# Layer 0 of a sparse graph network: the packed edges' own rows by a float32 one-hot product instead of by row fetches

## The chip, the cores and the metric

The kernel runs on one core of a Trainium2 chip. The metric is device time in microseconds (us) of one execution; a kernel is run several times and the median is told. The engines of the core work side by side, each through its own instructions in their order: PE (matmul; PEld is its weight load), DVE (vector), ACT (scalar, activation functions), POOL (here it issues indirect DMAs) and SP (issues plain DMAs). DMAs of all engines share 16 DMA engines.

## The reference, cut to what matters

Four layers work on x (4096 nodes, 64 features) with one adjacency matrix (4096 x 4096, an edge with probability 0.000976562, so about 4 edges a row). Each layer is x = x + layer(relu(layernorm(x))). Layer 0 is the one that is changed:

```
h = relu(layernorm(x))
left, right = logmap0(h) @ w_att[:64], logmap0(h) @ w_att[64:]
att[i, j] = sigmoid(left[i] + right[j] + b) * adj[i, j]
support[i] = sum_j att[i, j] * logmap(h[i], h[j])     # hyperbolic logarithm
x = x + proj(expmap(h, support))
```

logmap(h[i], h[j]) needs the products h[i].h[j], h[i].h[i] and h[j].h[j] and then only scalars, so an edge (i, j) costs the two rows h[i] and h[j], their dot product, and some 40 scalar operations. Layers 1 to 3 multiply the adjacency (as 8-bit floats) with 64 columns, on PE.

## The kernel before, in words

**Layer 0 by edges.** The function `neighbours` makes lists of edges and fetches rows of a table for them. The table `tab` has one row per node with TW = 69 columns: h (64), then scalars (1 + c x2, x2, right part, floor, left part). It lies in SBUF, as 32 tiles of 128 nodes, one node a partition, and a copy `rows_d` in HBM is what the fetches read.

**Stream.** 64 tiles of the transposed adjacency, 1 MB each, are loaded by SP into four buffers (`load`, L602). For each, ACT casts it to 8 bits (L800 for the first 24 tiles, which stay in SBUF; L803 for 40 tiles, which go through the buffers `f8` to HBM, L804, since SBUF is full of layer 0's tiles; they are loaded back at L1406 when layer 0 has ended), and PE packs it: the matmuls `pk` (L808) turn 16 rows of adjacency bits into one number. Eight tiles make a block: 512 nodes, in LB = 4 tiles of 128. After each half block ACT moves the packed words to `kt` (L814), PE transposes them (L818), and ACT copies a whole block's into `keyt` (L831).

**Lists (`lists`, one per block, NR = 8).** On DVE, eight-maximum and replace operations (L853 to L893) find a node's edges in the packed words. Up to NS = 4 edges of a node go to slots; `idx` (L879) holds the rows of their other ends, and `gather_slots` has POOL issue LB x NS = 16 indirect DMAs, one row per partition in each (`fetch`, L962), into `es`. Edges beyond the slots, up to NV = 24 a partition, are packed over partitions: PE counts them with a triangular matrix (`pb`, L901 and L902), DVE makes `mine` (L911), a one-hot matrix of 128 partitions by 512 places that tells from which partition each packed place takes its edge, and PE multiplies `mine` with the list's numbers (`pc`, L920 and L921). `mine` and the numbers are bfloat16, the numbers split into a high half `mvh` (L903) and a low half `mvl` (L904), two matmuls for each of NO = 4 columns of places. DVE then works out for each packed place `ovx`, the row of its edge's other end (L933), `own`, the row of the node it belongs to (L935, L936), and `rows_at`, where its result is to be added (L940, L941). `gather_packed` issues 2 x NO = 8 further fetches: 4 for `ovx` into `es`, 4 for `own` into `hi`.

**The rest of a block.** `chunk` forms the dot products: for the slots h is read from `tab` (L993), for the packed places from `hi` (L1005); ACT copies x2 and left of the nodes beside them (L999 from `tab`, L1003 from `hi`). `weights` computes the scalars of two blocks at a time (of the last two blocks one at a time), `sums` scales the fetched rows (L1115) and has PE add them up, `products`: slots with the identity (L1090), packed places with one-hot matrices `spot` (L1073, L1097). `dots` and `finish` end the layer for a group of rows (a group is two blocks; `finish` runs once for the first two groups and once for the last two), and write x (L1233). `row_stage` makes the table at the start, `row_rest` six small operations after it (L780 to L785) that only `finish` needs.

**The order.** Inside layer 0 the order of instructions on PE, DVE, ACT and POOL is fixed when the program is written. A planner runs a clock with assumed costs: each job is a generator that emits some instructions and yields their planned time in us on DVE (a bare number), PE or ACT, or the fetch queue ("FETCH"). STREAM_AT, PACE_MB and LATE say when tiles are assumed to arrive, ROWS_AT when the row stage has ended, PACE_DMA what a fetch costs (1.25), LANDED how long after the last fetch a chunk may be placed. Jobs are taken in the order of `kinds`, lists first if the fetch queue has under BACKLOG us of work. When PE has nothing planned, `fill` puts matmuls (L1083) that compute nothing of use there, into the PSUM bank `fill_t`.

Of the kernel before, what the change touches and what calls it, by code (L numbers as in the profile page):

```python
# [17 lines left out]
P = 128  # L18
# [32 lines left out]
STREAM_AT, PACE_MB, LATE = 8.0, 3.9, 3.0  # L51
ROWS_AT, PACE_DMA, LANDED, BACKLOG, SLOW, AHEAD, FILL = 46.0, 1.25, 3.0, 12.0, 1.05, 0.6, 0.75
EARLY = 3
# [524 lines left out]
def neighbours(ctx, tc, x_in, x, sh, adj_t, adj8, a8, over):  # L578
# [74 lines left out]
    V.tensor_scalar(upto, sh.diff, 0.0, None, op0=ALU.is_ge)  # L653


    mvh = [l0.tile([P, NV + 3], BF16, name=f"mvh{s}") for s in range(2)]
    mvl = [l0.tile([P, NV + 1], BF16, name=f"mvl{s}") for s in range(2)]
    for s in range(2):
        V.tensor_scalar_mul(mvh[s][:, NV + 1 : NV + 2], p_f, float(NCH))
        V.tensor_scalar_add(mvh[s][:, NV + 2 :], p_f, 1.0)  # L660

    def scalar(name):
# [60 lines left out]
    def row_stage(beside):  # L723
# [38 lines left out]
        V.tensor_scalar_mul(pn, x2, c_t)  # L762
        V.tensor_scalar(tab[:, :, D + 3], pn, NOISE2, RSQRT_MIN, op0=ALU.mult, op1=ALU.add)
        for m in range(NQ):
# [3 lines left out]
        V.tensor_mul(la, la, iv)  # L768
        V.tensor_mul(tab[:, :, D + 2], right, la)
        V.tensor_mul(left, left, la)  # L770
        V.tensor_scalar_add(tab[:, :, D + 4], left, sh.batt_t)
        nc.scalar.dma_start(rows_d[1:, :].rearrange("(p n) w -> p n w", p=P), tab)
# [5 lines left out]
    def row_rest():  # L778

        V.tensor_scalar(beta, x2, negc_t, 1.0, op0=ALU.mult, op1=ALU.add)  # L780
        V.tensor_scalar_max(clipb, beta, MIN_NORM)
        V.tensor_scalar_mul(fac, clipb, 3.0 / 16.0)
        V.tensor_mul(fb, fac, beta)
        V.reciprocal(rcb, clipb)
        V.tensor_scalar_mul(rcb, rcb, rc_t)  # L785


# [3 lines left out]
    def pack(u):  # L791
# [4 lines left out]
        for v in range(4):  # L796
            at = part * 4 + v
            a = load(b, at)
            if b < EARLY:
                S.copy(a8[b][:, 4 * at : 4 * at + 4, :], a, saturate=False)  # L800
            else:
                f8 = strm.tile([P, 4, 512], FP8, tag="f8", bufs=3, name=f"f8_{b}_{at}")
                S.copy(f8, a, saturate=False)  # L803
                nc.scalar.dma_start(adj8[b][:, 4 * at : 4 * at + 4, :], f8.bitcast(BF16))  # L804
            bits = a.bitcast(BF16).rearrange("p j (i b) -> p j i b", b=2)
            for j in range(4):
                w = 4 * v + j
                T.matmul(  # L808
                    pk, wflat[:, w * P : (w + 1) * P], bits[:, j, :, 1], start=(w == 0), stop=(w == 15),
                )  # L810
            if v < 3:
                yield
# [22 lines left out]
    ovx = [l0.tile([P, NO], U32, name=f"ovx{b}") for b in range(NR)]  # L835
    own = [l0.tile([P, NO], U32, name=f"own{b}") for b in range(NR)]
    rows_at = [l0.tile([P, NO], F32, name=f"rows_at{b}") for b in range(NR)]

    k16s = l0.tile([P, NR, LB, 16], F32, name="k16s")
    vfs = l0.tile([P, NR, LB, 16], F32, name="vfs")  # L840
    ovs = l0.tile([P, NR, NV], F32, name="ovs")
    ends = l0.tile([P, NR], F32, name="ends")
    BIG = 1.5 * 2.0**36

    def lists(nb):
        def tile_(tag, shape, dt=F32):
            return l0e.tile([P] + shape, dt, tag=tag, name=f"{tag}_{nb}")

        k16, vf, ov = k16s[:, nb], vfs[:, nb], ovs[:, nb]
        scr = tile_("scr", [NW])  # L850
# [44 lines left out]

        cnt, om, mh, ml = tile_("cnt", [1]), tile_("om", [NV]), mvh[nb % 2], mvl[nb % 2]
        V.tensor_scalar(om, ov, 0.0, None, op0=ALU.is_gt)
# [4 lines left out]
        T.matmul(pb[:, 1:2], upto, cnt, start=True, stop=True, skip_group_check=True)  # L902
        V.tensor_copy(mh[:, :NV], ov)  # L903
        V.tensor_sub(ml[:, :NV], ov, mh[:, :NV])  # L904
        yield 0.4
        yield "PE", 0.5

        at0, end = pb[:, 0:1], pb[:, 1:2]
        from_, mine = tile_("from", [512], BF16), tile_("mine", [512], BF16)
        V.tensor_scalar(from_, io, at0, None, op0=ALU.is_gt)  # L910
        V.scalar_tensor_tensor(mine, io, end, from_, op0=ALU.is_le, op1=ALU.mult)  # L911
        V.tensor_copy(mh[:, NV : NV + 1], at0)
        V.tensor_sub(ml[:, NV:], at0, mh[:, NV : NV + 1])
        V.tensor_copy(ends[:, nb : nb + 1], end)
        yield 1.7
        pc = psum.tile([P, 512], F32, tag="s", bufs=1, name=f"pc{nb}")
        pe = pc[:, : NO * (NV + 3)].rearrange("p (c e) -> p c e", c=NO)
        for c in range(NO):
            at = mine[:, c * P : (c + 1) * P]
            T.matmul(pe[:, c, :], at, mh, start=True, stop=False, skip_group_check=True)  # L920
            T.matmul(pe[:, c, : NV + 1], at, ml, start=False, stop=True, skip_group_check=True)  # L921
        yield "PE", 1.0

        tf, c1, kt_, rw, rw2 = (tile_(t, [NO]) for t in ("tf", "c1", "kt_", "rw", "rw2"))
        its = tile_("its", [NO, NV])
# [8 lines left out]
        V.tensor_scalar(kt_, c1, BIG, -1.0 / 8192.0, op0=ALU.subtract, op1=ALU.mult)  # L934
        V.scalar_tensor_tensor(rw, kt_, float(1 + LB * nb), pe[:, :, NV + 1], op0=ALU.add, op1=ALU.add)  # L935
        V.scalar_tensor_tensor(own[nb], tf, 0.0, rw, op0=ALU.is_gt, op1=ALU.mult)  # L936
        yield 0.9
        gather_packed(nb)
        yield "FETCH", PACE_DMA * 2 * NO
        V.scalar_tensor_tensor(rw2, kt_, float(P), pe[:, :, NV + 2], op0=ALU.mult, op1=ALU.add)  # L940
        V.scalar_tensor_tensor(rows_at[nb], tf, 0.0, rw2, op0=ALU.is_gt, op1=ALU.mult)  # L941
        yield 0.35

# [14 lines left out]
    NE = LB * NS + NO  # L958
    es, hi, s_e, x2e, lfe = {}, {}, {}, {}, {}

# [5 lines left out]
    def gather_slots(nb):  # L966
        g, q = divmod(nb, 2)
        if q == 0:
            es[g] = l0w.tile([P, 2, NE, TW], F32, tag="es", name=f"es{g}")
            hi[g] = l0w.tile([P, 2, NO, TW], F32, tag="hi", name=f"hi{g}")  # L970
        for k in range(LB):
            for s in range(NS):
                fetch(es[g][:, q, k * NS + s, :], idx[nb][:, k, s : s + 1])

    def gather_packed(nb):
        g, q = divmod(nb, 2)
        for c in range(NO):
            fetch(es[g][:, q, LB * NS + c, :], ovx[nb][:, c : c + 1])
        for c in range(NO):
            fetch(hi[g][:, q, c, :], own[nb][:, c : c + 1])  # L980

    def chunk(nb):
# [14 lines left out]
        )  # L997
        for dst, col in ((x2e, D + 1), (lfe, D + 4)):
            S.copy(  # L999
                dst[g][:, q, :ns].rearrange("p (k s) -> p k s", k=LB),  # L1000
                tab[:, tiles, col : col + 1].to_broadcast([P, LB, NS]),
            )
            S.copy(dst[g][:, q, ns:], own_[:, :, col])  # L1003
        yield 1.2
# [4 lines left out]
    def weights(se, e_g, x2i, lf, name, last):  # L1009
# [7 lines left out]

        xj, right, floor = e_g[:, :, :, D + 1], e_g[:, :, :, D + 2], e_g[:, :, :, D + 3]
        den, gap, pr, y, e, w = (tile_(t) for t in ("den", "gap", "pr", "y", "e", "w"))
# [56 lines left out]
    pieces = []  # L1076
    fill_t = psum.tile([P, 512], F32, tag="fill", name="fill_t")
    fill_in = io.bitcast(BF16)[:, :512]

    def fill(n):  # L1080

        for _ in range(n):
            T.matmul(fill_t, wflat[:, :P], fill_in, start=True, stop=True, skip_group_check=True)  # L1083
# [156 lines left out]
    with tc.manual_schedule(engines=engines):  # L1240
        units = [pack(u) for u in range(2 * NR)]
        packed = [0]
        clock = {"now": ROWS_AT, "FETCH": ROWS_AT + 6.0, "PE": 0.0, "ACT": 0.0}

# [21 lines left out]
        row_stage(pack_one)  # L1266
        row_rest()
        landed, freed, done = {}, {}, set()
# [18 lines left out]
        def freed_by(nb):  # L1287

            return [("sum", nb // 2 * 2 - 1)] if nb > 1 else []

        class Job:
            def __init__(self, kind, nb, gen, ready, end=None):
# [10 lines left out]

        kinds = ["chunk", "sum", "last", "spot", "list", "dots", "finish", "over"]
        queues = {k: [] for k in kinds}
        for nb in range(NR):
            g, q = divmod(nb, 2)
            queues["list"].append(Job("list", nb, lists(nb), list_ready, list_done))
            queues["chunk"].append(Job("chunk", nb, chunk(nb), landed.get))
            queues["spot"].append(Job("spot", nb, spots(nb), after(("list", nb), *freed_by(nb))))  # L1310
# [9 lines left out]
        for g0, g1 in ((0, NQ - 2), (NQ - 2, NQ)):  # L1320
            queues["finish"].append(Job("finish", g0, finish(g0, g1), after(*[("dots", g) for g in range(g0, g1)])))
        queues["over"].append(Job("over", 0, overflow(0), after(("list", NR - 1))))
# [454 lines left out]
```

## Time and profile before

| | us |
|---|---|
| median of 5 runs | 941.34 |
| lowest, highest | 940.16, 946.19 |
| the profiled execution: whole time | 947.1 |
| the profiled execution: span, first to last instruction | 945.2 |
| mean granted clock of TensorE in it | 0.897 of full |
| busy of the span: PE, PEld, DVE, ACT, POOL | 764.2, 569.2, 496.0, 343.7, 202.3 |
| first and last fetch on POOL begin | 61.99, 313.81 |
| last write of x in layer 0 ends (L1233) | 360.9 |

How to read it: times in the views count from the span's start. A row of a timeline gives start, duration, engine, line, operation, output <- inputs, shape, how often, and in brackets how long the engine had been idle and what ended that. The busy tenths have one digit for each of 40 equal slices. A row of the waits gives who waited for what: us in total, times, longest. A matmul with float32 operands shows as two records.

### The profile page before, as it was taken

How to read it: one execution, taken by the hardware profiler on the slowest of the kernel's cores; microseconds unless marked ns; L12 is line 12 of the kernel's file. 1: busy time of each engine (PE TensorE's matmuls, PEld its weight loads, DVE VectorE, ACT ScalarE, POOL GpSimd, SP SyncE). 2: the span in 40 equal slices, each digit the busy share in tenths (PEclk: the TensorE clock that was granted, in tenths of full speed). 3: DMA queues.
4: the chain of work that ended last, by engine and by line, in shares of the span. 5: the costliest groups of instructions: out<-in, count | busy, mean ns of one | idle time of the engine just before them, and what ended most of it. 6: DMA issues, size and time to landing. Idle time of an engine off the chain costs nothing.

```text
span 945.2 us, 15036 instructions
## 1 busy us (share of the span) xinstructions
PE 764.2 (81%) x6068; PEld 569.2 (60%) x6068; DVE 496.0 (52%) x1451; ACT 343.7 (36%) x471; POOL 202.3 (21%) x210
## 2 busy tenths in 40 slices
PE   4776766987767761789998999989958989989896
PEld 1332332734436441679998999989955656656564
DVE  4685667677788656445555222144443344444443
ACT  4764566486531422211111011122223334434342
POOL 0327777777777200000000000000000000000000
PEclk9889788689995775699999899999988999999999
DMA  8889799999921006300000000000000000000000
GB/s 277 316 292 358 237 375 365 289 360 384 348 52 27 9 2 283 162 2 1 1 2 1 1 1 1 1 2 2 1 1 1 1 12 1 1 12 1 12 2 15
DMA packets 49250, 99.53 MB, mean 105 GB/s; under 512 B 6802, under 2 KB 6802, under 8 KB 48274
## 3 DMA queue, kind: packets, MB, share of 16 engines
q1 hardware_dynamic: 35232, 79.70, 23.5%
q10 hardware_dynamic: 7794, 11.98, 3.5%
q0 software_dynamic: 6144, 6.80, 3.2%
q8 instruction: 49, 0.80, 0.3%
q14 instruction: 31, 0.25, 0.1%
HBM read 85.79 MB, written 12.67 MB: 104 GB/s over the span
## 4 chain that ended last, share of the span: by engine, by line
PE 61%; DVE 17%; DMA 7%; ACT 6%; POOL 5%; issue 4%; ACTq 0%; DVEq 0%; POOLq 0%; SPq 0%
PE l2a_acc L1482 9%; PE l2b_acc L1482 9%; PE l_acc L1611 9%; PE l_acc L1482 8%; PE cnt L1635 7%; PE cnt L1624 6%; POOL es L962 3%; DMA hi<-rows_d,own 3%; PE v L1097 2%; POOL hi L962 2%; DMA a<-in_adj_t 2%; PE pk L808 2%; PE fill_t L1083 2%; PE l_u L1442 1%; DVE scr L854 1%
## 5 line engine op out<-in xcount | busy, mean ns | idle before, releaser
L1482 PEld LDWEIGHTS <-a 128*128 128x128 fp8e4 x3072 | 264.6, 99 | 9.1 <-issue 6.9
L1631 DVE TENSOR_SCALAR wt<-cnt 128x512 int16<-128x512 f32 x128 | 88.5, 692 | 123.9 <-PE cnt L1624 123.9
L962 POOL DMA_INDIRECT es<-rows_d,idx x128 | 127.7, 998 | 59.0 <-issue 36.6
L1632 ACT ACTIVATE wt<-cnt,low_t 128x512 int16<-128x512 f32 x128 | 87.9, 687 | 137.8 <-PE cnt L1624 137.8
L1083 PE MATMUL fill_t<-io,wpack 128*128 128x512 bf16 x410 | 111.0, 412 | 0.0
L1611 PEld LDWEIGHTS <-wt 128*128 128x128 bf16 x1024 | 90.5, 99 | 32.2 <-issue 3.1
L1611 PE MATMUL l_acc<-y_b,wt 128*128 128x192 bf16 x1024 | 108.4, 250 | 0.0
L1635 PE MATMUL cnt<-a,fill 128*128 128x512 fp8e4 x248 | 82.1, 388 | 20.0 <-DVE wt L1631 20.0
L808 PE MATMUL pk<-a,wpack 128*128 128x512 bf16 x256 | 76.6, 425 | 22.7 <-DMA a<-in_adj_t 22.6
L1482 PE MATMUL l_acc<-y_a,a 128*128 128x193 bf16 x1024 | 93.6, 251 | 0.0
L1482 PE MATMUL l2a_acc<-y_b,a 128*128 128x192 bf16 x1024 | 89.3, 249 | 3.0 <-DVE y_b L1451 3.0
L1482 PE MATMUL l2b_acc<-y_a,a 128*128 128x192 bf16 x1024 | 88.2, 248 | 3.0 <-DVE y_a L1451 3.0
L803 ACT CAST f<-a 128x2048 fp8e4<-128x2048 f32 x40 | 75.8, 1896 | 16.7 <-DMA a<-in_adj_t 10.0
L1624 PE MATMUL cnt<-a,tri 128*128 128x512 fp8e4 x256 | 78.4, 388 | 0.0
L1083 PEld LDWEIGHTS <-wpack 128*128 128x128 bf16 x410 | 42.8, 106 | 49.5 <-issue 11.3
L808 PEld LDWEIGHTS <-wpack 128*128 128x128 bf16 x256 | 26.9, 106 | 60.0 <-issue 26.3
L800 ACT CAST a<-a 128x2048 fp8e4<-128x2048 f32 x24 | 45.0, 1896 | 10.6 <-DMA a<-in_adj_t 6.3
L1624 PEld LDWEIGHTS <-tri 128*128 128x128 bf16 x256 | 25.1, 98 | 37.7 <-issue 22.9
L1635 PEld LDWEIGHTS <-fill 128*128 128x128 bf16 x248 | 24.2, 98 | 27.9 <-issue 21.3
L1097 PEld LDWEIGHTS v<-es,spot 128*128 128x128 f32 x256 | 40.0, 244 | 1.0
L1097 PE MATMUL v<-es,spot 128*128 128x65 f32 x256 | 40.0, 327 | 0.0
L1429 PE MATMUL l_t<-ident,ln_h 128*128 128x128 f32 x48 | 8.3, 301 | 37.6 <-DVE ln_h L1714 37.6
(362 smaller groups left out, 803.5 us busy)
## 6 DMA issues: line engine op xcount, KB each, us to landing
a<-in_adj_t SPq DMA_DIRECT2D x64, 1024.0 KB, 9.5
adj<-f ACTq DMA_DIRECT2D x40, 256.0 KB, 6.3
a<-adj SPq DMA_DIRECT2D x5, 2048.0 KB, 16.5
es<-rows_d,idx POOLq DMA_INDIRECT x128, 5.5
rows_d<-tab ACTq DMA_DIRECT2D x1, 1104.0 KB
x<-in_x SPq DMA_DIRECT2D x1, 1024.0 KB
out<-z SPq DMA_DIRECT2D x4, 256.0 KB, 2.0
es<-rows_d,ovx POOLq DMA_INDIRECT x32, 5.4
```

The lines of the kernel that those rows point to most:

```text
L800: S.copy(a8[b][:, 4 * at : 4 * at + 4, :], a, saturate=False)
L803: S.copy(f8, a, saturate=False)
L808: T.matmul(pk, wflat[:, w * P : (w + 1) * P], bits[:, j, :, 1], start=(w == 0), stop=(w == 15),)
L962: G.indirect_dma_start(out=dst, out_offset=None, in_=rows_d, in_offset=bass.IndirectOffsetOnAxis(ap=at, axis=0))
L1083: T.matmul(fill_t, wflat[:, :P], fill_in, start=True, stop=True, skip_group_check=True)
L1097: T.matmul(pv[:, k * DQ : (k + 1) * DQ], spot[nb][:, c, k * P : (k + 1) * P], es[g][:, q, LB * NS + c, :DQ], start=False, stop=(c == NO - ...
L1482: T.matmul(acc, a8[n // 4][:, c, n % 4 * P : (n % 4 + 1) * P], y3[:, c, :cols], start=(c == first[0] and k % 2 == 0), stop=(c == last[-1] ...
L1611: T.matmul(accs[k // 2][:, k % 2, : 3 * D], wts[k // 4][:, (k % 4) * P : (k % 4 + 1) * P].bitcast(BF16), y3[:, c, : 3 * D], start=(c == NC ...
L1624: T.matmul(cnt[b], tri, masks[b], start=head_, stop=last, skip_group_check=True)
L1631: V.tensor_scalar(wts[0], cnt[0], -(128.0 - MAX_NEIGH) * UNIT, 0.0, op0=ALU.add, op1=ALU.max)
L1632: S.activation(wts[1], cnt[1], AF.Relu, bias=low_t)
L1635: T.matmul(cnt[b], fill, masks[b], start=False, stop=False, skip_group_check=True)
```

## The change

Own rows are not fetched. The product that sorts the list's numbers into places is made in float32 with `mine` in float32, one matmul for each column of places instead of two, and the same `mine` is multiplied with the table itself: for each column of places, 4 tiles of h (256 columns, the new job `own_rows`), and 4 tiles of two scalars, x2 and left (`ps`, in `lists`). A partition's place then has four candidates, one of each of the block's 4 tiles; the one-hot `of` picks one, by a multiply with it and a sum over the 4. The result is `hi`, now 66 columns. `own_rows` goes by two columns of places at a time through one PSUM bank, which it shares with the fillers ("w"): while PE's product waits to be read (`filled`), no filler is put in.

With it: the fetch queue is planned with NO instead of 2 x NO packed fetches; a chunk waits for `own_rows` of its block as well; `row_rest` becomes a job that comes after the list of block 1; two scalars of the table change columns; `from_` uses the buffer of `scr`; `f8` has 2 buffers instead of 3; ROWS_AT goes from 46 to 50, LANDED from 3 to 4.5, and the fetch clock's start from ROWS_AT + 6 to ROWS_AT + 5.

```diff
-ROWS_AT, PACE_DMA, LANDED, BACKLOG, SLOW, AHEAD, FILL = 46.0, 1.25, 3.0, 12.0, 1.05, 0.6, 0.75
+ROWS_AT, PACE_DMA, LANDED, BACKLOG, SLOW, AHEAD, FILL = 50.0, 1.25, 4.5, 12.0, 1.05, 0.6, 0.75
...
-                f8 = strm.tile([P, 4, 512], FP8, tag="f8", bufs=3, name=f"f8_{b}_{at}")
+                f8 = strm.tile([P, 4, 512], FP8, tag="f8", bufs=2, name=f"f8_{b}_{at}")
...
-        V.tensor_copy(mh[:, :NV], ov)
-        V.tensor_sub(ml[:, :NV], ov, mh[:, :NV])
-        yield 0.4
         yield "PE", 0.5
...
-        from_, mine = tile_("from", [512], BF16), tile_("mine", [512], BF16)
+        from_ = tile_("scr", [512], BF16)
+        mine = l0w.tile([P, 512], F32, tag="mine", name=f"mine{nb}")
         V.tensor_scalar(from_, io, at0, None, op0=ALU.is_gt)
         V.scalar_tensor_tensor(mine, io, end, from_, op0=ALU.is_le, op1=ALU.mult)
-        V.tensor_copy(mh[:, NV : NV + 1], at0)
-        V.tensor_sub(ml[:, NV:], at0, mh[:, NV : NV + 1])
+        V.tensor_copy(ovs[:, nb, NV : NV + 1], at0)
...
         for c in range(NO):
             at = mine[:, c * P : (c + 1) * P]
-            T.matmul(pe[:, c, :], at, mh, start=True, stop=False, skip_group_check=True)
-            T.matmul(pe[:, c, : NV + 1], at, ml, start=False, stop=True, skip_group_check=True)
-        yield "PE", 1.0
+            T.matmul(pe[:, c, :], at, ovs[:, nb, :], start=True, stop=True, skip_group_check=True)
+        for c in range(NO):
+            at = mine[:, c * P : (c + 1) * P]
+            T.matmul(
+                ps[:, c], at, tab[:, tiles, D + 1 : D + 3], start=True, stop=True, skip_group_check=True
+            )
+        yield "PE", 1.6
...
-        V.scalar_tensor_tensor(rw, kt_, float(1 + LB * nb), pe[:, :, NV + 1], op0=ALU.add, op1=ALU.add)
-        V.scalar_tensor_tensor(own[nb], tf, 0.0, rw, op0=ALU.is_gt, op1=ALU.mult)
-        yield 0.9
+        yield 0.6
         gather_packed(nb)
-        yield "FETCH", PACE_DMA * 2 * NO
+        yield "FETCH", PACE_DMA * NO
...
+        of = l0w.tile([P, NO, LB], F32, tag="of", name=f"of{nb}")
+        V.scalar_tensor_tensor(
+            of, bc(kt_, LB), 1.0, io[:, None, :LB].to_broadcast([P, NO, LB]), op0=ALU.add, op1=ALU.is_equal
+        )
+        hs_ = tile_("hs_", [NO, 2, LB])
+        V.tensor_mul(hs_, ps.rearrange("p c k e -> p c e k"), of[:, :, None, :].to_broadcast([P, NO, 2, LB]))
+        V.tensor_reduce(hi[g][:, q, :, D:], hs_, AX.X, ALU.add)
+        yield 1.0
+        mines[nb], ofs[nb] = mine, of
+
+    def own_rows(nb):
+
+        g, q = divmod(nb, 2)
+        mine, of = mines.pop(nb), ofs.pop(nb)
+        for c in range(0, NO, 2):
+            filled[0] = False
+            pw = psum.tile([P, 512], F32, tag="w", bufs=1, name=f"pw{nb}_{c}")
+            pw = pw.rearrange("p (c k d) -> p c k d", c=2, k=LB)
+            for i in range(2):
+                T.matmul(
+                    pw[:, i], mine[:, (c + i) * P : (c + i + 1) * P], tab[:, LB * nb : LB * nb + LB, :D],
+                    start=True, stop=True, skip_group_check=True,
+                )
+            yield "PE", 1.8
+            for i in range(2):
+                hw_ = l0e.tile([P, D, LB], F32, tag="hw_", name=f"hw_{nb}_{c + i}")
+                V.tensor_mul(
+                    hw_, pw[:, i].rearrange("p k d -> p d k"),
+                    of[:, c + i, None, :].to_broadcast([P, D, LB]),
+                )
+                V.tensor_reduce(hi[g][:, q, c + i, :D], hw_, AX.X, ALU.add)
+            filled[0] = True
+            yield 1.6
...
         for c in range(NO):
             fetch(es[g][:, q, LB * NS + c, :], ovx[nb][:, c : c + 1])
-        for c in range(NO):
-            fetch(hi[g][:, q, c, :], own[nb][:, c : c + 1])
...
-    fill_t = psum.tile([P, 512], F32, tag="fill", name="fill_t")
...
+        if not filled[0]:
+            return
+        fill_t = psum.tile([P, 512], F32, tag="w", bufs=1, name="fill_t")
...
-        row_rest()
...
+        def chunk_ready(nb):
+            return landed.get(nb) if ("own", nb) in done else None
...
-        kinds = ["chunk", "sum", "last", "spot", "list", "dots", "finish", "over"]
+        kinds = ["chunk", "sum", "last", "spot", "own", "list", "rest", "dots", "finish", "over"]
...
-            queues["chunk"].append(Job("chunk", nb, chunk(nb), landed.get))
+            queues["chunk"].append(Job("chunk", nb, chunk(nb), chunk_ready))
+            queues["own"].append(Job("own", nb, own_rows(nb), after(("list", nb))))
...
+        queues["rest"].append(Job("rest", 0, row_rest(), after(("list", 1))))
```

## The prediction

> **What bounds the kernel now.** I read four views: the busy tenths by slice, the tables by stretch, the waits, and the timelines around the end of layer 0. A slice is 945.2/40 = 23.6 us. Layer 0 is the first 15 slices, and the change lies wholly in it.
>
> ```profile
> DVE  4685667677788656445555222144443344444443
> POOL 0327777777777200000000000000000000000000
> DMA  8889799999921006300000000000000000000000
> ```
>
> POOL shows 7 tenths at most, but its rows last 0.94 us and begin 1.25 us apart, the rest being "issue": POOL is full from 62 us (its first fetch) to 315 us. That is 8 blocks of 16 + 4 + 4 fetches, 192 x 1.25 = 240 of 253 us. The stream's DMA (third line) is nearly full as well, until 264 us. So two queues run side by side at one pace: a block is 24 x 1.25 = 30.0 us of POOL, and 8 tiles of adjacency are 31.7 us (39 steps of the cast from 107.75 to 262.14, 3.96 each). Where the stream ends, POOL is hardly late:
>
> ```profile
> 262.14 1.88 ACT L803 CAST f<-a 128x2048 fp8e4<-128x2048 f32 x1
> 267.64 1.05 ACT L831 COPY keyt<-keys 128x512 f32<-128x512 f32 x2
> ...
> 278.80 0.17 DVE L879 TENSOR_SCALAR idx<-js 128x16 uint32<-128x16 f32 x1
> ...
> 280.36 1.01 POOL L962 DMA_INDIRECT hi<-rows_d,own  x1 [0.30 <-issue]
> 281.67 0.94 POOL L962 DMA_INDIRECT es<-rows_d,idx  x1 [0.30 <-DVE ovs L891]
> ...
> 308.87 1.15 POOL L962 DMA_INDIRECT hi<-rows_d,own  x1 [0.30 <-issue]
> ...
> 313.81 0.94 POOL L962 DMA_INDIRECT hi<-rows_d,own  x1 [0.30 <-issue]
> ...
> 317.15 0.42 DVE L1005 TENSOR_TENSOR pd<-es,hi 128x256 f32<-128x256 f32 x1 [5.72 <-DMA hi<-rows_d,own]
> ```
>
> The reader is to see that the last block's list could be fetched from 279.0, is fetched from 281.7 because block 6's own rows are still queued, and that the eighth and last wait of DVE for own rows ends at 317.15. From there the end of layer 0 is a chain: two sums' weights, the products on PE (to 343.9), finish on DVE (to 360.9), layer 1. Layers 1 to 3 need another 584 us, bound by PE and untouched; they start when layer 0's last x is written, so what layer 0 saves or loses at its end passes through whole. The waits name the other cost of the own rows:
>
> ```profile
> ACT x2e L1003 <- DMA hi<-rows_d,own: 31.3, 7, 9.6
> ...
> DVE pd L1005 <- DMA hi<-rows_d,own: 22.8, 6, 5.8
> PE pb L901 <- DVE cnt L898: 21.2, 4, 10.1
> ```
>
> ACT and DVE, which run in order, stand before own rows, and PE stands behind DVE. In 90 to 100 us that leaves DMA at a share of 0.67 and PE with 0.60 us of work.
>
> **Removed: 32 fetches.** 32 x 1.25 = 40 us of POOL. Most of it buys nothing, because the stream comes at 31.7 us a block; what counts is the end. The last block's fetches then start at about 279.3. 20 of them end their issue 19 steps later: 23.8 us at the clean step of 1.25, 26.6 at the 1.40 that the 23 steps of this execution took (281.67 to 313.81). Landing took 3.2 us (313.81 to 317.0). So the packed rows are there at 306.3 to 309.1 instead of 317.0: **8 to 11 us earlier, I take 9**. The list words for the packed fetch were ready at 296 (L933), well ahead of POOL in either case.
>
> **Added on DVE.** Per block, own_rows has 4 multiplies of 128x256 (row L1005: 0.42, next start after 0.46) and 4 reductions to 64 (96 elements take 0.25, 512 take 0.69, so 256 some 0.42): 4 x 0.85 = 3.4 us. The three small operations on ps add 0.5; the split into two bfloat16 halves and the own index go (L903, L904, L912 or L913, L935, L936: 0.8). Net 3.1 a block, 25 us in all. The multiply reads PSUM; rows L927 and L928, the same 128x96 from SBUF and from PSUM, took 0.26 and 0.25, so I add nothing. [...] mine in float32 instead of bfloat16: L911 took 0.76 for bfloat16 and L733's 512 float32 elements 0.69, so between 0.1 less and, at twice the bytes, 0.7 more; I take 0. DVE is busy 24.3 and 24.6 of 30 us in 250 to 280 and 280 to 310: two own_rows (6.8 us) fit there only because 13.7 us of waiting for fetches and PE (3.69, 0.37, 0.83, 0.28, 0.74, 2.09, 5.72) lie in 255 to 317. Fits, but full: I charge **2 us**. row_rest (1.4 us, 49.7 to 51.1) moves behind list 1, into such idle time: list 0 waits on ACT's keyt, not on it, so nothing comes or goes.
>
> **Added on PE.** Per block, 4 float32 products with 256 columns. The nearest row is this:
>
> ```profile
> L1090 PE MATMUL v<-es,ident x64: 380/381/781, 157.4 to 340.0; 128*128 128x260 f32 x64
> ```
>
> 64 records are 32 products, two passes each: 0.76 us at full clock, 1.56 at the half clock of the longest. So 3.0 to 6.2 a block. The list product goes from 8 bfloat16 matmuls (67.62 to 67.97) to 8 float32 ones of 26 and 8 columns; from L1097 (65 columns, 16 products in 3.53 or 7.07) they are at most 0.22 to 0.44 each, 1.8 to 3.5. Net 4.5 to 9 a block. The cover is filler: fill_t ran 410 times, 111 us, only to keep PE going, and is now left out while pw is held. Without that cover each block would put 4.5 to 9 us between pk products, and the stream with it. The rows show the half clock after idle time (10 us without work to 99.4; then fill_t takes 0.42 a matmul, not 0.22). [...] Here the fillers give way to real work on the same engine; were block 7's own products and its sums (5.4 us in this execution, 10.3 for block 6's) both at half clock, the tail would be 8 us longer.
>
> DVE's wait for pc (0.4 to 0.8) grows by 1 to 3 us a list. Queued behind it are chunks and sums. POOL, fed 20 us ahead by idx, covers it.
>
> **Removed waits, added waits.** The copies of own x2 and left (L1003) no longer wait for a DMA: 31.3 us of ACT, 22.8 of DVE. But the chunk still waits for the packed rows, queued 5 us earlier, and is placed 1.5 us later by the planner (LANDED). The DMA share fell below 1.05 by 0.38, 0.21, 0.21 and 0.11 in the four stretches of 10 us at 90, 100, 170 and 180: 9 us of stream at most to be won, if nothing else stops it. New: a filler behind pw waits for DVE's multiply, with pk behind it on PE; each wait is as long as DVE lags the plan, 0 to 3 us (the waits on chunks were 3 to 8).
>
> **f8 with two buffers instead of three.** A cast must wait for the store of the tile two before:
>
> ```profile
> L804 ACTq DMA_DIRECT2D adj<-f x40: 326/327/400, 109.7 to 264.1; - x40
> ...
> DMA to landing us min/median/max: 2.0/6.3/7.4
> ```
>
> Cast 1.9 + landing 6.3 + 0.1 is 8.3 for two tiles, 4.15 a tile against 3.96: 39 x 0.19 = 7.4 us of stream, behind which the last list stands. With the store at 2.0 us (an empty queue, the last one) it is nothing; at 7.4, 29 us. A cast that is held back holds back loads, and so shortens the store's queue; I take **+2**, and the freed waits at **-3**: the stream ends about as before.
>
> **Behind the last chunk.** The weights of block 6 stood still at 309.6 behind DVE's wait and went on at 319.0. Its products ran 324.68 to 335.2, fillers to 338.5, then block 7's, whose scaled rows had been ready at 332.1:
>
> ```profile
> 324.68 3.80 PE L1090 MATMUL v<-es,ident 128*128 128x260 f32 x8 [6.88 <-issue]
> 328.28 6.92 PE L1097 MATMUL v<-es,spot 128*128 128x65 f32 x32
> 335.00 3.65 PE L1083 MATMUL fill_t<-io,wpack 128*128 128x512 bf16 x10
> 338.48 1.92 PE L1090 MATMUL v<-es,ident 128*128 128x260 f32 x8
> ```
>
> If block 6 is done first, up to 6 us go. DVE and PE have block 7's own_rows there instead, so I take **0 to -4, and write -2**.
>
> **Sum**: -9 + 2 + 2 - 3 - 2 = -10 us. The profiled execution took 947.1 (span 945.2 and 1.9 around it), so 937.1 for one like it; it stands 5.8 over the median, so 941.3 - 10 = **931 us**.
>
> **Rivals.**
> - *More: the stream is freed too.* If the lost DMA share comes back (half to all of 9 us) and block 6 gets out of the way, 920 to 926. For: PE's 10 us waits behind DVE. Against: the two f8 buffers.
> - *Nothing at the end: the hand-offs eat it.* Block 7's own_rows follow the list (297): two rounds of PE 1.5 to 3 us, DVE 1.7 and hand-off 0.4 to 0.8, 304 to 308, beside a landing at 306 to 309. If DVE is late with other work there by 6 to 9 us, the own rows end last instead of the fetch: 937 to 945.
> - *Slower: the store of f8 sets the stream.* The last list starts as late as the stream ends. The gain without this term, 12, is used up and 5 us more lost when 39 x ((2.0 + L)/2 - 3.96) passes 17, at a landing L of 6.8 us: over the median now, under the longest. At 7.4 the time is 941 - 12 + 29 = 958; between, 946 to 958. For: DMA at 1.05 for most of the stream. Against: the relief by held loads; the early tiles (24 of 64) write no store.
> - *It doesn't do what it says*: excluded for the fetches; the call is gone from the code.
>
> **Chances.** Forecast (926 to 936.6) 0.45; more 0.19; nothing 0.20; slower 0.16. A measurement of this kernel tells about 0.5% from no change, 4.7 us: faster 0.64, same 0.20, slower 0.16. The range reaches from the freed stream's 920 to 946, where the slower case begins.
>
> **What would show it.** After: 160 POOL fetches, the last block's about 5 us apart from its chunk's second multiply, at 306 to 310 us; no DMA wait at the x2e copies; POOL with gaps between blocks; products' end at 331 to 336. Wrong if the last cast starts after 270 with waits "DMA adj<-f" ahead of it, if PE waits for DVE's multiply before fillers by more than 3 us at a time, or if the chunk's multiply waits for own_rows.

## The result, and the profile after

The changed kernel takes **948.4 us** (median of 29 runs, 942.82 to 959.84), the kernel before, beside it, 942.34 (50 runs, 938.1 to 948.22). The ratio, of the means without the three runs over 958 us, is 1.0069, its 95% interval 1.0052 to 1.0086: slower by some 6 us, where 10 us less were forecast. The profiled execution of after took 947.85 us, its span is 946.0. Two of the five sets of runs below fell on two chips on which the kernel before takes 998.21 and 993.52 us; each ratio is to the kernel before on the same chip.

The slices of after (23.65 us each), to be set beside those of before:

```profile
DVE  4668678667889976545555222134443444444443
POOL 0337675266367300000000000000000000000000
DMA  8889999899811004500000000000000000000000
```

POOL has the gaps that were expected, and DMA isn't freer: the stream still fills 11 slices. The end of layer 0, from the timelines (start, duration, engine, line; in brackets the idle time before):

```profile
262.72 1.90 ACT L796 CAST f<-a 128x2048 fp8e4<-128x2048 f32 x1
267.19 1.08 ACT L824 COPY keyt<-keys 128x512 f32<-128x512 f32 x2 [0.53 <-PE keys L811]
...
281.37 0.42 DVE L854 MAX8 k16s<-keyt 128x8 f32<-128x256 f32 x1
...
290.47 0.17 DVE L880 TENSOR_SCALAR idx<-js 128x16 uint32<-128x16 f32 x1
...
316.42 0.94 POOL L997 DMA_INDIRECT es<-rows_d,ovx  x1 [0.30 <-issue]
...
324.11 0.42 DVE L975 TENSOR_REDUCE hi<-hw 128x64 f32<-128x256 f32 x1
324.49 1.23 DVE L1025 TENSOR_TENSOR pd<-es,tab 128x1024 f32<-128x1024 f32 x1
325.63 0.42 DVE L1037 TENSOR_TENSOR pd<-es,hi 128x256 f32<-128x256 f32 x1
```

The last cast and the copy of block 7's keys come at the times of before (262.14 and 267.64). But DVE starts the last list 13 us after its keys are there, and idx is ready at 290.47 instead of 278.80. Until then it is busy with the second part of list 6, which begins (L887; L886 in the kernel before) 9 us later than in the kernel before and takes 13.5 us instead of 11:

```profile
267.89 0.35 DVE L887 TENSOR_TENSOR rem<-cand,j 128x192 f32<-128x192 f32 x1
...
281.27 0.19 DVE L951 TENSOR_REDUCE hi<-hs__6_2503 128x8 f32<-128x32 f32 x1
```

and before:

```profile
258.81 0.35 DVE L886 TENSOR_TENSOR rem<-cand,j 128x192 f32<-128x192 f32 x1
...
269.78 0.42 DVE L853 MAX8 k16s<-keyt 128x8 f32<-128x256 f32 x1
```

From idx on the change does gain: chunk 7's second multiply follows 35.2 us after idx instead of 38.4, without a wait for a DMA, and the last x 39.1 us after that instead of 43.0 (364.77 against 360.19). 12.1 lost ahead of the list's end, 3.2 and 3.9 won behind it, 0.4 won ahead of the keys: layer 0 ends 4.6 us later.

Who held up the stream stands in the waits (us in total, times, longest), first of after, then of before:

```profile
ACT f L796 <- DMA adj<-f: 52.5, 22, 4.5
```

```profile
ACT f L803 <- DMA adj<-f: 3.3, 2, 2.0
```

And the transposes behind them, and the stores, in after:

```profile
PE keys L811 <- ACT kt L807: 48.3, 16, 8.0
```

```profile
L797 ACTq DMA_DIRECT2D adj<-f x40: 325/398/400, 101.7 to 264.7; - x40
...
DMA to landing us min/median/max: 2.0/6.2/7.2
```

The stored casts wait 52.5 us for stores instead of 3.3. PE waits 48.3 us for kt in this stretch (8 to 345 us; 30.4 before), since kt stands in ACT's order behind a cast that waits. The first stored cast starts at 99.73, 8 us earlier than before, the last at 262.72: 4.18 us a tile, against 3.96. So the lead with which the stream came to the first store was used up tile by tile. The store itself is as quick as before (6.2 against 6.3).

### The profile page after: what moved, and what is told of

Same layout as the page of the kernel before. It is cut to its first block, busy times and chain, and to the rows that moved or that the text cites. A ratio compares the mean times of both kernels' runs of the same rounds, so it can differ in the third digit from the quotient of the medians.

```text
span 946.0 us, 15065 instructions
## 1 busy us (share of the span) xinstructions
PE 779.6 (82%) x6096; PEld 578.2 (61%) x6096; DVE 518.6 (55%) x1496; ACT 343.4 (36%) x471; POOL 169.0 (18%) x178
## 4 chain that ended last, share of the span: by engine, by line
PE 62%; DMA 14%; DVE 11%; ACT 10%; issue 2%; ACTq 0%; SPq 0%
DMA adj<-f 10%; PE l2b_acc L1520 9%; PE l2a_acc L1520 9%; PE l_acc L1649 9%; PE l_acc L1520 8%; PE cnt L1673 7%; PE cnt L1662 6%; ACT f L796 4%; PE fill_t L1117 3%; DMA a<-in_adj_t 2%; PE v L1131 2%; PE pk L801 1%; PE v L1124 1%; ACT a L793 1%; PE l_u L1480 1%
## 5 line engine op out<-in xcount | busy, mean ns | idle before, releaser
L1117 PE MATMUL fill_t<-io,wpack 128*128 128x512 bf16 x310 | 101.2, 423 | 14.4 <-DVE hw L971 9.6
L796 ACT CAST f<-a 128x2048 fp8e4<-128x2048 f32 x40 | 75.8, 1896 | 54.0 <-DMA adj<-f 52.5
L1117 PEld LDWEIGHTS <-wpack 128*128 128x128 bf16 x310 | 32.4, 108 | 70.6 <-issue 41.4
L801 PEld LDWEIGHTS <-wpack 128*128 128x128 bf16 x256 | 27.5, 110 | 48.6 <-issue 17.0
L811 PE MATMUL keys<-ident,kt 128*128 128x128 f32 x64 | 15.5, 388 | 48.3 <-ACT kt L807 48.3
L811 PEld LDWEIGHTS keys<-ident,kt 128*128 128x128 f32 x64 | 10.0, 193 | 57.0 <-ACT kt L807 57.0
L1673 PEld LDWEIGHTS <-fill 128*128 128x128 bf16 x248 | 24.0, 97 | 28.0 <-issue 21.3
```

The costliest lines, as they stand in the source:

```text
L801: T.matmul(pk, wflat[:, w * P : (w + 1) * P], bits[:, j, :, 1], start=(w == 0), stop=(w == 15),)
L811: T.transpose(banks[b][k // 2][:, k % 2, part * P : part * P + P], kt[:, k * P : (k + 1) * P], sh.ident)
L1673: T.matmul(cnt[b], fill, masks[b], start=False, stop=False, skip_group_check=True)
```

## The experiments

Three theories: **R**, the ring of two store tiles holds up the stream; **O**, own rows' work on DVE and PE stands ahead of the lists; **P**, the planner's new constants place the lists late.

**1. The ring alone, in the kernel before**, run twice.

```
-                f8 = strm.tile([P, 4, 512], FP8, tag="f8", bufs=3, name=f"f8_{b}_{at}")
+                f8 = strm.tile([P, 4, 512], FP8, tag="f8", bufs=2, name=f"f8_{b}_{at}")
```

> The kernel before with one edit: two f8 buffers instead of three. Theory R (the store ring sets the stream): the casts of the 40 stored tiles go from 3.96 to 4.15 or 4.2 us apart, ACT waits 30 to 55 us for stores instead of 3.3, keys and lists come later, and the kernel is 4 to 10 us slower than before (946 to 952). Theory O (the own rows' work on DVE and PE, ahead of the lists, makes the last list late): within 2 us of before (940 to 944).

> The kernel before with two fp8 store tiles instead of three, and nothing else; every engine keeps its order. It is asked again because on the chip of the first four runs every kernel, the one before included, took about 998 us, with stalls of 5 to 17 us that no wait explains. Theory R (the store ring of two makes the casts wait for stores, the keys come late behind them, and the last lists with them): ratio to before 1.004 to 1.010, casts waiting for a store 30 us or more in all. Theory O (own rows' work on DVE and PE stands ahead of the lists): ratio 0.998 to 1.003, and the waits of the casts for stores stay under 20 us. Theory P (the planner's new constants put the pieces of the lists later): 0.998 to 1.003.

The first pair of times, 997.29 against 998.21, ratio 1.0 (0.9966 to 1.0034), is from the chip that takes 998 us. There ACT stood still in places where no wait is recorded, this once for 14.84 us:

```profile
84.29 0.69 ACT L814 ACTIVATE kt<-pk,num 128x512 f32<-128x512 f32 x1 [14.84 <-issue]
```

The stored casts were 4.67 us apart there, more than a ring of two asks for; they waited 24.5 us for stores, but the ring cost nothing that the interval shows. On a chip where the kernel before takes 940.75 it was 950.04: ratio **1.011** (1.0073 to 1.0148), on R's side and just above what R gave (1.004 to 1.010). The waits:

```profile
ACT f L803 <- DMA adj<-f: 42.1, 25, 4.0
```

Casts 4.24 us apart, the last at 272.9 us instead of 262.1. Every engine's order is that of before, so this is the ring and nothing else.

**2. Three store tiles in the changed kernel**, run three times.

```
-                f8 = strm.tile([P, 4, 512], FP8, tag="f8", bufs=2, name=f"f8_{b}_{at}")
+                f8 = strm.tile([P, 4, 512], FP8, tag="f8", bufs=3, name=f"f8_{b}_{at}")
...
-        mine = l0w.tile([P, 512], F32, tag="mine", name=f"mine{nb}")
+        mine = l0w.tile([P, 512], F32, tag="mine", bufs=1, name=f"mine{nb}")
```

> The changed kernel with three f8 buffers again; room is made by one buffer instead of two for mine, the order of all instructions stays. Theory R: the 52.5 us of ACT behind stores go, the last list's fetch starts 5 to 9 us earlier than 290.9, and the kernel is 5 to 12 us faster than the changed one, at or under before (934 to 943). Theory O: within 3 us of the changed kernel (945 to 951), the last list still 9 us or more behind its keys.

> The changed kernel with three fp8 store tiles (the tile of the slots' owners, mine, has one buffer in place of two, to make room); every engine keeps its order. Theory R: ratio to before 0.996 to 1.001, the wait of the casts for stores back under 10 us, idx of block 7 fetched at or before 283 us. Theory O: 1.005 to 1.008 as the change itself, idx of block 7 at 288 to 292. Theory P: the same as O.

> The changed kernel with three fp8 store tiles (one buffer of mine), asked again so that the other three kernels can be set against it on the same chip. Theory R, which two chips have borne out so far (ratio 0.988 and 1.005): 0.985 to 1.002, always 1.2 to 2 per cent below the kernel with two tiles on an ordinary chip.

On the chip of 998 us the ratio was 1.0047 (1.0013 to 1.0081), no gain, with casts 4.48 us apart. On the others 930.54 against 940.75, **0.9884** (0.985 to 0.9917), and 930.58 against 941.52, **0.9864** (0.9828 to 0.9901): a larger gain than R had given (0.996 to 1.001). The casts wait for loads again, as they should in a stream; this row is of the second of the three:

```profile
ACT f L796 <- DMA a<-in_adj_t: 27.2, 23, 2.1
```

The step is 3.73 us (97.6 to 243.0), in the third run 3.67 (96.4 to 239.6). So the change with the third tile left to it beats the kernel before by 10 to 11 us, and the ring of two costs it 18 (948.4 to 930.5).

**Control for the one buffer of mine**, which made the room: two store tiles, one buffer of mine.

> Control for the run with three f8 buffers: the changed kernel with one buffer for mine and still two f8 buffers. Both theories: same as the changed kernel within 2 us (946 to 950); if it is slower, the run with three f8 buffers pays for its one mine buffer too.

> Control: the changed kernel with one buffer of mine in place of two, which the kernels with three store tiles also have; two store tiles as in the change, every engine in the same order. If the gain with three store tiles is the ring's: ratio to before 1.004 to 1.011, as the change itself. If it is the buffer of mine: 0.985 to 0.995.

1.0061 (1.0022 to 1.01) and 1.0099 (1.0065 to 1.0133), on the chips of 998 and 993 us. It gains nothing there, but on the first of them the third store tile gained nothing either, so this alone does not settle it. The last run of experiment 6 does: it has three store tiles and both buffers of mine (with lists first), and takes 0.988 of the kernel before on an ordinary chip. So the gain isn't mine's.

**3. One store tile in the kernel before**, for the size of R.

> The kernel before with one fp8 store tile in place of three; every engine keeps its order. It tests the size of theory R: with n tiles a stored cast can't come sooner than (cast 1.90 + store 6.2)/n after the one before it: 2.7 us at three, 4.05 at two (4.18 to 4.24 measured in two kernels), 8.1 at one. Theory R: step between stored casts 7.4 to 8.4 us (the store may land sooner when the DMA queues are emptier), last cast at 400 to 435 us, ratio to before 1.13 to 1.19. If the wait has another cause than the ring: a step of 4.2 to 5.

Ratio 1.0519 (1.0462 to 1.0576) on the chip of 993 us, casts 6.24 us apart on average, the last at 359.4 us: a miss in size. Some of the casts:

```profile
284.66 1.90 ACT L803 CAST f<-a 128x2048 fp8e4<-128x2048 f32 x1 [2.18 <-DMA adj<-f]
291.10 1.90 ACT L803 CAST f<-a 128x2048 fp8e4<-128x2048 f32 x1 [4.53 <-DMA adj<-f]
297.58 1.90 ACT L803 CAST f<-a 128x2048 fp8e4<-128x2048 f32 x1 [3.43 <-DMA adj<-f]
304.01 1.90 ACT L803 CAST f<-a 128x2048 fp8e4<-128x2048 f32 x1 [3.50 <-DMA adj<-f]
```

6.4 us apart, each waiting for its predecessor's store: the mechanism holds, but the store is done some 4.5 us after the cast (6.4 - 1.9), not 6.2. The landing that was read with several stores under way, and a load stream at 4 us a tile, did not carry over to one store at a time at 6.4 us a tile. Which of the two differences shortened it is not shown.

**4. The fetches alone: the kernel before without own fetches**, run twice.

```
-        for c in range(NO):
-            fetch(hi[g][:, q, c, :], own[nb][:, c : c + 1])
+        V.memset(hi[g][:, q, :, :], 1.0)
```

> The kernel before without the 32 fetches of own rows (192 POOL DMAs become 160): the own rows' tile is set to one by one DVE instruction for each block, so the attention of the overflowing slots is computed on wrong rows. It prices the fetches alone. If the gain of the change with three store tiles (ratio 0.988) comes from the fetches: ratio to before 0.980 to 0.992, the step between stored casts 3.7 to 3.8 us in place of 3.96. If it comes from something else in the change (index arithmetic, order, the constants): 0.993 to 1.002 and a step of 3.9 to 4.0 us.

> The kernel before without the 32 fetches of own rows (their tile is set to one by one DVE instruction for each block, so the attention of the overflowing slots is computed on wrong rows). It prices the fetches alone; on a chip where the kernel before takes 993 us it gave a ratio of 0.9685. If the fetches are what the change gains by: ratio 0.965 to 0.990 on an ordinary chip too, stored casts 3.7 to 3.8 us apart, and no wait for the rows of the own fetches. If most of 0.9685 belongs to that chip: 0.990 to 0.998.

0.9685 (0.9635 to 0.9735) on the chip of 993 us, and 916.25 against 941.52 on an ordinary one, **0.9732** (0.9706 to 0.9758): 25 us for 32 fetches. The step between casts is 3.63 us (101.6 to 243.3), block 7's keys are copied at 247.71 instead of 267.64, chunk 7 follows its idx after 31.7 us instead of 38.4:

```profile
243.28 1.88 ACT L803 CAST f<-a 128x2048 fp8e4<-128x2048 f32 x1
...
247.71 1.05 ACT L831 COPY keyt<-keys 128x512 f32<-128x512 f32 x2
```

In the profiled executions, 19.9 of the 31.8 us by which layer 0 ends earlier are there when the keys are: most of the gain is the stream's.

**5. Own rows' work taken out of the change**, with two store tiles and, run twice, with three.

```
-            pw = psum.tile([P, 512], F32, tag="w", bufs=1, name=f"pw{nb}_{c}")
...
-                T.matmul(
...
-                V.tensor_mul(
...
-                V.tensor_reduce(hi[g][:, q, c + i, :D], hw_, AX.X, ALU.add)
+            V.memset(hi[g][:, q, c : c + 2, :D], 1.0)
```

> The changed kernel without own rows' products on PE and without their multiplications and sums on DVE: the 34 first columns of the packed own rows are set to one instead, so the attention of the overflowing slots is computed on wrong rows; the pieces keep their places in the planned order. It takes away 32 products of fp32, 32 multiplications and 32 sums. Theory O: ratio to before 0.985 to 0.997 (some 10 to 20 us less than the change: the list of block 7 ends 10 us or more earlier, chunk 7 follows it). Theory R: 1.000 to 1.006, since the casts still wait for the ring of two, 30 us or more. Theory P: 1.000 to 1.006.

> The changed kernel with three store tiles and one buffer of mine, without own rows' products, multiplications and sums (the packed own rows are set to one, so the attention of the overflowing slots is computed on wrong rows). It prices own rows' work on PE and DVE where the stream is free. Theory O (that work delays the last list and chunk 7): ratio to before 0.975 to 0.985, chunk 7's second multiplication at 292 to 300 us in place of 304.6. If the work lies beside waits: 0.985 to 0.990 and chunk 7 at 302 to 306.

> The changed kernel with three store tiles, without own rows' products, multiplications and sums (the packed own rows are set to one, so the attention of the overflowing slots is computed on wrong rows). Against the kernel with three tiles on the same chip: theory O (own rows' work on PE and DVE is still on the path) 5 to 12 us less, chunk 7's second multiplication at 292 to 300 us; if that work lies beside waits, within 3 us, chunk 7 at 301 to 306.

The edit sets all 64 columns of h, not 34 as the first of these texts says.

Two tiles: 945.83, 1.0043 (1.001 to 1.0076), the casts still waiting 52.8 us for stores. Three tiles: 0.9864 (0.9817 to 0.9912) on the chip of 993 us, and 929.98 beside 930.58 with the work in: the 32 products, 32 multiplications and 32 sums cost nothing that can be measured (the intervals of the two ratios, 0.9823 to 0.9896 and 0.9828 to 0.9901, nearly coincide). The amount of that work, theory O's first form, is out.

**6. The plan.** The old constants in the change, and the lists ahead of own rows in `kinds`.

```
-ROWS_AT, PACE_DMA, LANDED, BACKLOG, SLOW, AHEAD, FILL = 50.0, 1.25, 4.5, 12.0, 1.05, 0.6, 0.75
+ROWS_AT, PACE_DMA, LANDED, BACKLOG, SLOW, AHEAD, FILL = 46.0, 1.25, 3.0, 12.0, 1.05, 0.6, 0.75
...
-        clock = {"now": ROWS_AT, "FETCH": ROWS_AT + 5.0, "PE": 0.0, "ACT": 0.0}
+        clock = {"now": ROWS_AT, "FETCH": ROWS_AT + 6.0, "PE": 0.0, "ACT": 0.0}
```

> The changed kernel with the planner's three constants of before (rows at 46.0, landing 3.0, fetch clock +6.0), so that pieces are emitted in another order on every engine. Theory P: ratio to before 0.993 to 1.002, the list of block 7 ends 5 us or more earlier than in the changed kernel. Theories R and O: 1.003 to 1.012, no earlier end of the list of block 7.

> The changed kernel with own rows placed after lists in the planner's order of kinds. Theory R: same as the changed kernel within 3 us (945 to 951), since stores still hold the casts. Theory O: lists are no longer cut by own rows, the last list's fetch starts 4 to 8 us earlier than 290.9, and the kernel is 3 to 7 us faster than the changed one (941 to 945).

> The changed kernel with three store tiles (three buffers of the input block in place of four, to make room, and two of mine), with the pieces of a list put ahead of own rows' pieces in the planner's order of kinds. With two store tiles that order gave a ratio of 1.0227 where the change had about 1.006, as own rows' work then stands between the last list and its chunk. If that is what counts: 3 to 15 us more than the kernel with three tiles. If theory O holds for the lists: 3 to 10 us less, list 7 ended by 275 us.

The old constants: 956.16, 1.0151 (1.0107 to 1.0195), so theory P falls; the new ones suit the change better. Lists first: 1.0227 (1.0173 to 1.0282) with two tiles on the chip of 998 us, which neither theory had, 930.94 with three on an ordinary one, 0.988 (0.9854 to 0.9907), as without: block 7's list ends earlier (idx at 264.1 us instead of 267.8) and layer 0 does not (last x 343.4 against 340.9).

**7. What is between 930 and 916?** Both kernels lack own rows' work and own fetches (5 and 4). One run gives the kernel before, without its fetches, the new constants; the other takes own rows' places out of the changed plan:

```
-        for c in range(0, NO, 2):
-            filled[0] = False
-            yield "PE", 1.8
-            V.memset(hi[g][:, q, c : c + 2, :D], 1.0)
-            filled[0] = True
-            yield 1.6
+        V.memset(hi[g][:, q, :, :D], 1.0)
+        yield 0.3
```

> The kernel before without the 32 fetches of own rows (their tile set to one, so the attention of the overflowing slots is computed on wrong rows), and with the planner's three constants of the change (rows at 50.0, landing 4.5, fetch clock +5.0). The kernel without own fetches took 916 us, the changed kernel with three store tiles and without own rows' work 930; this run and the next ask what the 14 us between them are. If the constants are it: ratio to before 0.982 to 0.990. If not: 0.968 to 0.978, as without them.

> The changed kernel with three store tiles, without own rows' work (the packed own rows set to one by one DVE instruction, so the attention of the overflowing slots is computed on wrong rows), and now also without the places that this work holds in the plan: the generator of a block's own rows is one piece of 0.3 us in place of four pieces that sum to 6.8 us of planned time. If the places of own rows' pieces in the plan (they push the chunk of the block before into the middle of a list, where DVE waits for its rows) are the 14 us: ratio to before 0.968 to 0.979. If it is the rest of the change (fp32 owners, their two kinds of products, the later row table): 0.983 to 0.990.

914.69, 0.9711 (0.9685 to 0.9737), and 931.33, 0.9866 (0.9823 to 0.991), against 941.31. It isn't the constants, and taking the places out does not bring the 14 us back; by the ranges of the expectation this speaks for the rest of the change. The profiled executions, stage by stage:

| us | step between stored casts | block 7's keys copied at | from there to idx | to chunk 7 | to the last x |
|---|---|---|---|---|---|
| before | 3.96 | 267.6 | 11.2 | 38.4 | 43.0 |
| before, no own fetches (4) | 3.63 | 247.7 | 12.2 | 31.7 | 36.8 |
| the same, new constants | 3.67 | 243.5 | 15.8 | 30.5 | 38.4 |
| after | 4.18 | 267.2 | 23.3 | 35.2 | 39.1 |
| after, three tiles (third run) | 3.67 | 243.1 | 24.6 | 34.0 | 39.1 |
| the same, no own work (5) | 3.70 | 248.0 | 22.8 | 33.7 | 41.3 |
| the same, no places either | 3.69 | 255.8 | 13.6 | 35.2 | 43.6 |

With own rows ahead of lists in the plan, block 7's list takes 23 to 25 us behind its keys, whether the work is done or not; without, 11 to 16. That looks as if the list's 12 us were those of the order, but the last row does not show it. Its idx is ready at 269.4, 1.4 us earlier than in the row above (270.8); the stretch is shorter because its keys come 7.8 us later. In the three-tile kernels of the change idx is ready between 264 and 271 us, own rows in the plan or not, in the two kernels of before without own fetches at 259 to 260. DVE's timeline of list 6, in the change with three tiles, shows an interruption:

```profile
228.30 0.41 DVE L971 TENSOR_TENSOR hw<-pw,of 128x256 f32<-128x256 f32 x1
...
233.44 0.42 DVE L971 TENSOR_TENSOR hw<-pw,of 128x256 f32<-128x256 f32 x1
...
235.18 1.23 DVE L1025 TENSOR_TENSOR pd<-es,tab 128x1024 f32<-128x1024 f32 x1
237.01 0.43 DVE L1037 TENSOR_TENSOR pd<-es,hi 128x256 f32<-128x256 f32 x1 [0.60 <-DMA es<-rows_d,ovx]
...
240.27 0.17 DVE L880 TENSOR_SCALAR idx<-js 128x16 uint32<-128x16 f32 x1
```

The list began at 224.37; two rounds of block 5's own rows and block 5's chunk, with a wait for its fetched rows, come before its idx at 240.27, 15.9 us later. In the kernel of the last row of the table that is gone, and list 6 has its idx after 8.9 us, but its stored casts began at 104.9 us instead of 97.8 and its tail, from idx on, is 4 us longer: there is no gain. What puts its stream late was not taken apart. Left of the change there are the list's products in float32 (pc keeps PE busy for 21.3 us over 8 blocks in the last of these runs, for 5.6 in the kernel before) and row_rest behind list 1; neither was tried alone. DVE's waits for that product don't settle it: 15.5 us in the kernel of 916, 9.0 in the change with three tiles. The cause of these 14 us stays open.

## Why the prediction was wrong

**The step that failed is "f8 with two buffers instead of three", taken at +2 us; it measured 18.** Its arithmetic was right: 4.15 us a tile were worked out, 4.18 measured. Two things were wrong with it. The 7.4 us it gave were cut to 2 because a cast that is held back "shortens the store's queue"; the landing stayed at 6.2, and in the kernel before alone the ring costs 9.3 (experiment 1). And the floor was compared with the step of before, 3.96, which was itself held up by the own fetches: without them the stream runs at 3.63 to 3.73. Against that pace the floor costs 39 x (4.18 - 3.67) = 20 us, and 18 were measured (experiment 2). The rival "slower" had this mechanism, but put its threshold at a landing of 6.8 us, for the same reason; it came true at 6.2.

**The sum beside the runs.** Forecast were -14 for the fetches with their waits and the end, +2 for the work on DVE, +2 for the ring: -10. Measured were -25 for the fetches (experiment 4), +14 for the rest of the change, its cause open (7), and +18 for the ring (2): +7, where the medians differ by 6. That the change with three tiles, at 930.5, lands on the forecast's 931 is luck: a gain priced 11 us too low and a cost of 14 us against the 2 that were charged nearly cancel.

**"Removed waits", -3**, was mis-sized as well, in the other direction. The bound of 9 us was read from the DMA share. Without own fetches block 7's keys are copied 19.9 us earlier (experiment 4): 39 x 0.33 = 13 from the step, 6 from an earlier first stored cast. ACT's 31.3 us of waiting for own rows stood in front of casts in its order. Without these fetches the DMA share rose from 0.94 to 1.05 (90 to 150 us) and from 0.99 to 1.05 (150 to 210 us), so the stream had room. How much of the gain is ACT's waits and how much the DMA time of the fetches themselves was not separated. Of the stretch from 90 to 100 us, too, the reading was off: DVE's wait there, 7.83 us in front of L1005, ended with the slots' rows and not with own rows.

**"Removed: 32 fetches", -9.** From idx to chunk 7 it measured 6.6 less in experiment 4, but 3.2 in the change: the last fetch was issued at 316.42, which by the 3.2 us of before lands at 319.6, and the chunk's second multiply came at 325.63, directly behind own rows' second half (322.75 to 324.53). That looks like the rival "nothing at the end", own rows ending last. But ahead of that half DVE was busy with block 6's weights and `spot` from 314.73 on, and with own rows' work taken out chunk 7 still follows its idx after 33.7 us (34.0 with it, both with three tiles). So some 6 us are lost to what stands ahead of the chunk in DVE's order, and own rows' work is not what makes them. The wait that ended at 317.15 is called the eighth in the prediction; the view counts six. The whole gain of the fetches, 25 us, was nearly twice what the sum gave them with the waits and the tail (14).

**"Added on DVE", +2**: 0.6 measured, within the noise. The durations were right: multiplies 0.42, reductions 0.42. A source in PSUM made no measurable difference at this size either: L971, from PSUM, has a median of 0.424 us, L1037, the same 256 elements from SBUF, of 0.420 (L1005 in the kernel before: 0.426). **"Added on PE", 0**, held for own rows (experiment 5): pw took 0.38 us a pass, 0.80 at the longest, and fillers waited at most 2.9 us for DVE, their weight loads 3.5. There were 310 fillers instead of 410, and the mean granted clock was no lower for it, 0.907 against 0.897. The list's product in float32 was not priced alone. **"Behind the last chunk", -2**: 3.9 in the change.

**Missing from the sum**: what the added pieces do to the order of DVE. I had charged their microseconds, and found idle time to put them in. In the change the last list ends 12 us later behind its keys than before, whether own rows' work is done or not. That the places of own rows' pieces cause it is not shown: the last run of experiment 7 does not bear it out.

Of the signs named beforehand, 160 fetches, no DMA wait at the x2e copies and POOL's gaps came true, though the gain they were to show did not follow; the chunk's second multiply, forecast for 306 to 310 us, came at 325.63. "Last cast after 270" was not met (262.72) while the waits "DMA adj<-f" were there: the sign was set by the pace of before, as the step was. The layers behind differ too: 584.3 us from layer 0's end in before's profiled execution, 580.5 in after's, so the two profiled executions lie 0.75 us apart and the medians 6.1.

## What to carry to other kernels

A ring of n buffers sets a floor of (work + landing)/n for a stream (here, with two, 4.15 us a tile worked out and 4.18 and 4.24 measured; with one, 8.1 worked out and 6.24 measured, as the store was done sooner); compare it with the pace that the stream will have when the rest of the change has taken effect, not with today's. When memory for a new tile is taken from a ring, run that ring's size by itself in the old kernel first: one number in one line gave here the price that the prediction had wrong. And where the order is written out, look at what an added piece stands in front of, not only how long it is; here a list was cut up by such pieces, and with the cut gone the time stayed the same.

## What the runs showed of the hardware

The landing of a 256 KB store was 6.0 to 6.5 us (medians) with rings of two and three on the ordinary chips and 2.0 at the least; with one store at a time, on the chip of 993 us and in a slower stream, some 4.5 by the casts. And two chips ran the kernel before at 993 and 998 us instead of 941, with ACT and DVE idle for up to 18.5 us at a time where the records show no wait ("issue") or an unknown queue ("remote"); in the profiles of before and after, idle time of these two put down to "issue" is 0.2 us at the longest, and "remote" does not occur. On these chips the stream's step was 4.2 to 5.0 us with two or three store tiles. On the one of 998 us, at a step of 4.67, two tiles for three cost nothing measurable in the kernel before, where the same edit cost 1.1% on an ordinary chip. What stalls those engines was not found.
